# A twelve-sublayer decoder on one core: a written order of four engines for the fourth sublayer, loads by group in the first, and the channel attention's scores at the end of a drain step

## The chip, the cores and the metric

The kernel runs on one core of a Trainium2 chip. Five engines take part, each with an instruction queue of its own that it works through in order: TensorE (PE, with its weight loads shown as PEld), VectorE (DVE), ScalarE (ACT), GpSimd (POOL) and SyncE (SP), which here only issues DMA transfers. They wait for each other through semaphores. The metric is the device time of one execution in microseconds (us), the median of several runs. The profiler records one more execution; its span is the time from the first to the last instruction.

## The reference

A decoder of four layers with three sublayers each works on 64 sequences of 64 tokens with 256 features, 4096 tokens in all, next to a context of the same shape. Each sublayer is followed by a residual add and a layer norm. All is float32 unless said otherwise. Only these four sublayers matter here (`_softmax` and the casts left out):

```
x = _layernorm(x + L0_attn(x))        # 1: 16 query heads of 16, one key and value head, causal
    q = x @ q_w.T + q_b;  k = x @ k_w.T + k_b;  v = x @ v_w.T + v_b
    attn = softmax(where(causal, -inf, q k^T / 4));  out = (attn v) @ o_w.T + o_b
x = _layernorm(x + L0_xattn(x, ctx))  # 2: channel attention, no weights
    scaled = einsum('bsd,bse->bde', x, ctx) / 16
    attn = softmax(scaled, axis=1);  out = einsum('bde,bse->bsd', attn, ctx)
x = _layernorm(x + L0_ffn(x))         # 3: silu(x Wg) * (x Wu), then Wd; integer weights with scales
x = _layernorm(x + L1_attn(x))        # 4: attention over the 128 channels of one head
    k = x @ Wk + bk;  v = x @ Wv + bv                   # (64, 128) for each sequence
    scores = v k^T / 128;  attn = softmax(scores)       # per sequence, 64 x 64
    out = (attn v), repeated for 16 heads;  out = out @ Wo + bo
```

The sixteen heads of sublayer 4 are copies of one another, so the kernel adds the sixteen blocks of Wo once and multiplies by their sum (`wo`). Sublayers 5 to 12 are left as they are by the change.

## The kernel before

**Tiling.** Tokens are cut into 8 groups of 512 (NTOK), and each group into 4 tiles of 128 rows (TG), a tile being two sequences. X[g] holds a group's activations in SBUF during the whole program. CT[g] is the context transposed, `cns[g]` the context by rows. Weights and the context rows take slots of a ring of 8 buffers of 128 x 2048 numbers (`weight`, L323): a slot can be taken again when its last reader is done.

**Who sets the order.** A planner lays every engine's queue at compile time by its own estimate of costs. Inside `with self.tc.manual_schedule(engines=...)` the named engines keep the order of the program text. The first sublayer (`l0_attn`, L706) and the second and third, which run as one (`l0_both`, L839), name PE, ACT, DVE and POOL. The fourth (`l1_attn`, L980) names PE alone: ACT, DVE and POOL are laid by the planner there. SP is named nowhere. The next one, `l1_xattn`, names PE, ACT and DVE; everything from `l1_ffn` on names PE alone.

**Loads.** `run` (L351) issues all at the start in this order: x of group 0, the weights of the first sublayer, x of groups 1 to 7, ctxT of all groups. `l0_attn` then loads the row `l0_ob` and, through `context` (L742), the context rows of all groups. The transfers go through SP's queue. Each x, ctxT and ctx load of a group moves 512 KB.

**First sublayer.** Steps i = 0 to 37 work on 32 tiles, each tile in several stages: `scores` at step i, `probabilities` at i+1 (DVE sums, POOL multiplies at L649), `turned` at i+2 (PE transposes `pt`, ACT copies), `values` and `output` at i+3, `ended` at i+4. `prepare(g+1)` is spread over the four steps of group g in four parts; its `keys_values` sends v through a DMA to the other half of the partitions (`vs`, L600), and `queries` lets POOL add the bias row (`xb`, L605) and copy v and vs into `vbd` (L610). When the tiles are used up (i from 32) the steps of the drain already hold the channel attention of group 0: `next_scores`, `next_divided`, `next_values`, four tiles, a step each. `next_scores` writes the PSUM tile `s` of which there is one, DVE takes the maximum (L483), and ACT the exponentials (L489). It stands near the start of a step, ahead of `values`.

**Third sublayer.** `l0_both` goes through 48 units (8 groups of 6 slices of the hidden layer): `hidden(u)`, `down(u - 2)`, and between them the channel attention of the next group. At steps 36 and 39 DVE adds the blocks of Wo (`l1_output_weight`, L877).

**Fourth sublayer.** For each group: `rows_turned` (8 transposes into two banks, one copied by ACT, one by DVE; POOL adds the bias row to X as `xb`, L915), `keys_values` (kT and vT, L925, ACT adds the biases), `scores` (L936, a mask added by a bf16 matmul, DVE maximum, four ACT exponentials with row sums; `v` is vT turned), `turned` (pt, DVE copies), `values` (ot, ACT copies), `output` (o, L972, in two PSUM banks for four tiles; DVE makes z = o * sm + xb tile by tile, L974, then bn_stats, bn_aggr), and the norm: DVE L228, POOL's power -1/2 (L230), DVE nmr (L286), four ACT applies into X[g] (L288). PE's text order of a step is xt(i), pt(i-2), s(i-1), v(i-1), kv(i), ot(i-2), o(i-2): three groups are in flight. The banks: three shared by xt, pt, v and ot (`tr`), two `kv`, one `s`, two `acc`. Then `l1_xattn` begins with matmuls on rows that went through DRAM (L1046, L327), whose results DVE reduces (L1078).

Of the kernel before, what the change touches and what calls it, by code (L numbers as in the profile page):

```python
# [195 lines left out]
class Decoder:  # L196
# [154 lines left out]
    def run(self, layers):  # L351
        tc, nc, ctx = self.tc, self.nc, self.ctx
        self.const = self.pool(ctx, "const", 1)
        self.smallp = self.pool(ctx, "small", 4)
        self.xpool = self.pool(ctx, "xpool", 1)
        self.ring = self.pool(ctx, "ring", 8)

        self.X, self.CT, self.l3_rows = [], [], []
        for g in range(self.n_groups):
            xg = self.xpool.tile([P, TG, D], F32, tag=f"x{g}", name=f"x{g}")  # L360
            self.load(xg, self.ins["x"][g * NTOK : (g + 1) * NTOK, :].rearrange("(t p) d -> p t d", p=P))
            self.X.append(xg)
            if g == 0:
                self.l0_weights()
        self.constants()
        for g in range(self.n_groups):
            ct = self.xpool.tile([P, 2, NTOK], F32, tag=f"ct{g}", name=f"ct{g}")
            self.load(
                ct, self.ins["ctxT"][:, g * NTOK : (g + 1) * NTOK].rearrange("(c p) n -> p c n", p=P)
            )  # L370
            self.CT.append(ct)

        steps = [
            self.l0_attn, self.l0_both, self.l1_attn, self.l1_both,
            self.l2_l3, self.l3_xattn, self.l3_ffn,
        ]
        for n in layers:
            with ExitStack() as lctx:
                self.psum = self.pool(lctx, f"psum{n}", 2, space=PSUM, reuse_waits="tile")
                steps[n](lctx)  # L380
        for g in range(self.n_groups):
            for t in range(TG):
                at = g * NTOK + t * P
                nc.sync.dma_start(out=self.out[at : at + P, :], in_=self.X[g][:, t, :])

# [146 lines left out]
    def l0_attn(self, ctx):  # L532
# [161 lines left out]
        self.cns = [self.context(g) for g in range(self.n_groups)]  # L694
# [11 lines left out]
        with self.tc.manual_schedule(engines={E.PE, E.Activation, E.DVE, E.Pool}):  # L706
# [3 lines left out]
            for i in range(n + TG + 2):  # L710
# [3 lines left out]
                if i < n:  # L714
                    g, t = tiles[i]
                    if t == 0 and g + 1 < self.n_groups:
                        parts = prepare(g + 1)
                    state[i, "s"] = scores(g, t)
                elif i < n + TG:
                    next_scores(0, i - n)  # L720
                if 1 <= i <= n:
                    probabilities(state[i - 1, "s"])
                elif n < i <= n + TG:
                    next_divided(0, i - n - 1)
# [6 lines left out]
                if i < n:  # L731
                    exponentials(state[i, "s"])
                if behind:
                    behind()
                if 3 <= i <= n + 2:
                    state[i - 3, "ps"] = output(*tiles[i - 3], state.pop((i - 3, "o")))
                if i >= n + 2:
                    ends.extend(next_values(0, i - n - 2))
            for part in ends:
                part()  # L740

    def context(self, g):  # L742

        if g % 2 == 0:
            self.cn = self.weight("cn").rearrange("p (g t d) -> p g t d", g=2, t=TG)
        cn = self.cn[:, g % 2]
        self.load(cn, self.ins["ctx"][g * NTOK : (g + 1) * NTOK, :].rearrange("(t p) d -> p t d", p=P))
        return cn

    def l0_both(self, ctx):  # L750
# [88 lines left out]
        with self.tc.manual_schedule(engines={E.PE, E.Activation, E.DVE, E.Pool}):  # L839
            turn(0)  # L840
            for u in range(-1, len(units) + 2):
# [15 lines left out]
                if u in (HC * 6, HC * 6 + 3):  # L857
                    self.l1_output_weight(u == HC * 6)
            for part in ends:
                part()  # L860
# [15 lines left out]

    def l1_output_weight(self, first):  # L877
# [3 lines left out]
        if first:  # L881
            nc.vector.tensor_reduce(wo, raw[0], AX.X, ALU.add)
        else:
            nc.vector.tensor_reduce(half, raw[1], AX.X, ALU.add)
            nc.vector.tensor_tensor(wo, wo, half, ALU.add)

    def l1_attn(self, ctx):
# [3 lines left out]
        nc, ins = self.nc, self.ins  # L891
        DH = 128
        wk = self.pool(ctx, "l1a", 2)
# [3 lines left out]
        ident = wk.tile([P, P], BF16, tag="ident", name="ident", bufs=1)  # L897
        nc.vector.tensor_copy(ident, self.ident)
        mask = wk.tile([P, TG, P], BF16, tag="mask", name="mask", bufs=1)
        nc.vector.tensor_copy(mask, self.same.unsqueeze(1).broadcast_to([P, TG, P]))  # L900
        flat = lambda a: a.rearrange("p t n -> p (t n)")
        state = {}
# [4 lines left out]
        def rows_turned(g):  # L907
            xt = wk.tile([P, 2, NTOK], F32, tag="xt", name="xt")
            for c, copy in enumerate((nc.scalar.copy, nc.vector.tensor_copy)):
                ps = ring("xt")  # L910
                for t in range(TG):
                    nc.tensor.transpose(ps[:, t * P : (t + 1) * P], self.X[g][:, t, c * P : (c + 1) * P], self.ident)
                copy(xt[:, c, :], ps)
            xb = wk.tile([P, TG, D], F32, tag="xb", name="xb", bufs=3)
            nc.gpsimd.tensor_tensor(xb, self.X[g], bo.unsqueeze(1).broadcast_to([P, TG, D]), ALU.add)  # L915
            state[g] = xt, xb

        def keys_values(g):
            xt, xb = state[g]
            out = []  # L920
            for name, w_, b_ in (("kT", wkk, bk), ("vT", wvv, bv)):
# [5 lines left out]
                out.append(t_)  # L927
            state[g] = *out, xb

        def scores(g):  # L930

            kT, vT, xb = state[g]
# [6 lines left out]
            nc.tensor.matmul(ps, ident, flat(mask), start=False, stop=True, skip_group_check=True)  # L939
            s, sm = wk.tile([P, TG, P], F32, tag="s", name="s"), self.small(TG, "sm4")  # L940
            self.softmax_rows(s, ps.rearrange("p (t i) -> p t i", t=TG), TG, 1.0 / DH, sm)
            nc.vector.reciprocal(sm, sm)
# [5 lines left out]
            state[g] = s, sm, v, xb  # L948

        def turned(g):  # L950
            ps = ring("pt")
            for t in range(TG):
                nc.tensor.transpose(ps[:, t * P : (t + 1) * P], state[g][0][:, t, :], self.ident)
            pt = wk.tile([P, TG, P], F32, tag="pt", name="pt")
            nc.vector.tensor_copy(flat(pt), ps)
            return pt

        def values(g, pt):
            v, ps = state[g][2], ring("ot")
# [4 lines left out]
            return ot  # L964

        def output(g, ot):
            _, sm, _, xb = state.pop(g)
            z = wk.tile([P, TG, D], F32, tag="z", name="z")
            for t in range(TG):
                if t % 2 == 0:  # L970
                    ps = self.psum.tile([P, 2, D], F32, tag="acc", name="o", bufs=2)
                nc.tensor.matmul(ps[:, t % 2, :], ot[:, t * P : (t + 1) * P], wo, start=True, stop=True)  # L972

                nc.vector.scalar_tensor_tensor(  # L974
                    z[:, t, :], ps[:, t % 2, :], sm[:, t : t + 1], xb[:, t, :], ALU.mult, ALU.add
                )
            self.normalized(self.X[g], z)

        n = self.n_groups
        with self.tc.manual_schedule(engines={mybir.EngineType.PE}):  # L980
            for i in range(n + 2):
                if i < n:
                    rows_turned(i)
                if i >= 2:
                    pt = turned(i - 2)
                if 1 <= i <= n:
                    scores(i - 1)
                if i < n:
                    keys_values(i)
                if i >= 2:  # L990
                    output(i - 2, values(i - 2, pt))
# [1247 lines left out]
```

## Time and profile before

| what | us |
|---|---|
| median of 3 runs | 4510.14 |
| lowest and highest | 4506.65 and 4511.18 |
| the profiled execution's own time | 4513.13 |
| its span | 4511.4 |
| first sublayer, to the last step of its tiles (0 to 226.70) | 226.7 |
| its drain with the first channel attention (226.70 to 262.40) | 35.7 |
| second and third sublayer (262.40 to 605.80) | 343.4 |
| fourth sublayer, to its last apply (605.80 to 741.50) | 135.7 |
| PE busy in the whole span | 4118.9 (91%) |
| DVE, ACT, POOL busy | 3091.6, 2018.8, 1474.4 |

The profile has several views. The page gives busy times and groups of instructions. The timeline of an engine gives its instructions in order of time: start, duration, engine, line of the kernel (L...), operation, output<-input and shapes, and in brackets how long the engine had been idle before it and what released it. The windows view gives busy time of every engine in chosen stretches. PEclk is the share of PE's full clock that was granted. A float32 matmul shows as two instructions, so a group's four transposes of one kind can appear as x4 or x8.

### The profile page before, as it was taken

To read this page: it belongs to the slowest core of one execution; us is meant where nothing else is said; L and a number is where in the kernel's file an instruction comes from. 1 tells how busy PE (TensorE), PEld (TensorE's weight loads), DVE (VectorE), ACT (ScalarE), POOL (GpSimd) and SP (SyncE) were. 2 spreads that over 40 slices of the span, in tenths; PEclk is the share of its full clock that TensorE was granted. 3 is DMA by queue.
4 is the path that set the end of the run, shared out by engine and by line. 5 is a ranking of instruction groups with operands and counts; after the bars stand their busy time and mean duration, and the time that the engine had idled before them with its cause. 6 is when DMAs were issued, how large, how long until landed. Compare 5 with 4: busy or idle time off the path is not lost. (4 is left out here: it accounts for less than half of the span.)

```text
span 4511.4 us, 73874 instructions
## 1 busy us (share of the span) xinstructions
PE 4118.9 (91%) x28808; PEld 2662.9 (59%) x28808; DVE 3091.6 (69%) x6222; ACT 2018.8 (45%) x3662; POOL 1474.4 (33%) x1498
## 2 busy tenths in 40 slices
PE   7989988989988999839999999999979999999898
PEld 4645555666665555526666666666646666666566
DVE  5844536888665577767777777777757776777676
ACT  4655533767523566534444444444423322233444
POOL 3411111132431111015555555555523333333111
PEclk8989997999999999969999999999989999999999
DMA  4000011333200000011111111111210000000000
GB/s 142 3 20 10 5 48 33 69 82 69 65 1 21 1 1 1 10 47 29 27 27 29 27 27 29 24 29 29 65 56 10 10 10 10 10 11 12 7 16 17
DMA packets 99685, 128.26 MB, mean 28 GB/s; under 512 B 14916, under 2 KB 72452, under 8 KB 97928
## 3 DMA queue, kind: packets, MB, share of 16 engines
q1 hardware_dynamic: 99336, 123.53, 10.9%
q8 instruction: 228, 3.74, 0.3%
q14 instruction: 121, 0.99, 0.1%
HBM read 61.87 MB, written 19.42 MB: 18 GB/s over the span
## 5 line engine op out<-in xcount | busy, mean ns | idle before, releaser
L230 POOL TENSOR_TENSOR hrq<-hrq,neg_half 128x4 f32<-128x4 f32 x256 | 270.7, 1058 | 512.4 <-DVE hrq L228 512.3
L230 POOL TENSOR_TENSOR rstd<-rstd,neg_half 128x4 f32<-128x4 f32 (+1 forms) x168 | 148.2, 882 | 684.6 <-DVE rstd L228 599.3
L1078 DVE TENSOR_REDUCE mc<-sq 128x2 f32<-128x512 f32 x512 | 317.1, 682 | 64.2 <-PE sk L1076 63.6
L1084 ACT ACTIVATE e<-sk 128x512 f32<-128x512 f32 x512 | 265.2, 607 | 112.8 <-PE sk L1076 111.9
L230 POOL TENSOR_TENSOR hrk<-hrk,neg_half 128x4 f32<-128x4 f32 x160 | 187.8, 1174 | 291.0 <-DVE hrk L228 280.6
L1073 PE MATMUL sq<-l1x 32*128 32x256 f32 x2048 | 275.4, 406 | 1.6 <-DVE mc L1078 1.6
L1580 PE MATMUL p<-l3a_wq,xt 128*128 128x512 f32 x512 | 244.4, 601 | 9.9 <-DVE v L217 9.9
L1076 PE MATMUL sk<-l1x 32*128 32x256 f32 x2048 | 252.6, 393 | 0.5 <-DMA l1x<-l1x_m 0.5
L1580 PE MATMUL p<-l3x_wq,xt 128*128 128x512 f32 x512 | 238.2, 609 | 13.9 <-DVE k L1889 13.7
L1580 PE MATMUL p<-l3a_wk,xt 128*128 128x512 f32 x512 | 247.2, 606 | 0.0
L1073 PEld LDWEIGHTS sq<-l1x 32*128 32x128 f32 x2048 | 209.1, 194 | 55.4 <-issue 24.5
L1970 PE MATMUL acc<-l3x_wo,yt 128*128 128x256 f32 x1024 | 238.0, 386 | 0.7 <-ACT yt L215 0.7
L1580 PE MATMUL p<-l3a_wv,xt 128*128 128x512 f32 x512 | 234.5, 601 | 0.8 <-DVE k L217 0.4
L1787 PE MATMUL acc<-l3a_wproj,yt 128*128 128x256 f32 x1024 | 232.6, 381 | 0.0
L1787 PEld LDWEIGHTS acc<-l3a_wproj,yt 128*128 128x128 f32 x1024 | 195.1, 191 | 52.8 <-issue 29.1
L1970 PEld LDWEIGHTS acc<-l3x_wo,yt 128*128 128x128 f32 x1024 | 189.6, 190 | 28.0 <-ACT yt L215 0.9
L1076 PEld LDWEIGHTS sk<-l1x 32*128 32x128 f32 x2048 | 188.8, 187 | 7.2 <-issue 2.5
L1881 ACT ACTIVATE sq<-q 128x512 f32<-128x512 f32 x128 | 80.7, 630 | 207.3 <-DVE q L1889 154.4
L1580 PEld LDWEIGHTS p<-l3x_wq,xt 128*128 128x128 f32 x512 | 97.7, 196 | 126.6 <-issue 116.3
L1771 POOL TENSOR_TENSOR hry<-hry,neg_half 128x8 f32<-128x8 f32 x64 | 106.2, 1659 | 193.4 <-DVE hry L1767 193.4
L236 PEld LDWEIGHTS qT<-ident,q 128*128 128x128 f32 x1024 | 119.1, 141 | 77.3 <-issue 64.6
L1112 PE MATMUL ret<-e,vt 128*32 128x256 f32 x2048 | 140.5, 390 | 19.6 <-DVE mc L1078 18.6
(383 smaller groups left out, 10247.2 us busy)
## 6 DMA issues: line engine op xcount, KB each, us to landing
vs<-v SPq DMA_DIRECT2D x320, 128.0 KB
x<-in_x SPq DMA_DIRECT2D x8, 512.0 KB
ct<-in_ctxT SPq DMA_DIRECT2D x8, 512.0 KB
cn<-in_ctx SPq DMA_DIRECT2D x8, 512.0 KB
l1x<-in_ctx SPq DMA_DIRECT2D x128, 32.0 KB
l1x_x<-x SPq DMA_DIRECT2D x8, 512.0 KB
l1x<-l1x_x SPq DMA_DIRECT2D x128, 32.0 KB
l1x_r<-r SPq DMA_DIRECT2D x128, 32.0 KB
```

The costliest lines, as they stand in the source:

```text
L230: nc.gpsimd.tensor_tensor(out, out, self.neg_half[:, :n], ALU.pow)
L236: self.nc.tensor.transpose(ps[:, j * P : (j + 1) * P], blk, self.ident)
L1073: nc.tensor.matmul(ps[:, n, :], x_[rows, j, part], c_[rows, j, :], start=True, stop=True)
L1076: nc.tensor.matmul(ps[:, n, :], c_[rows, j, part], x_[rows, j, :], start=True, stop=True)
L1078: nc.vector.tensor_reduce(mc[new % 2][:, ra + k, 2 * j : 2 * j + 2], ps, AX.X, ALU.max, negate=True)
L1084: nc.scalar.activation(es[rb + k], ps, AF.Exp, scale=scale)
L1112: nc.tensor.matmul(ret[32 * r : 32 * r + 32, :], vt[i % 2][:, lc, 4 * r + j, :], es[r][:, lc, :], start=lc == 0, stop=lc == 1,)
L1580: self.nc.tensor.matmul(ps, lhs(c), w(c, cols), start=c == 0, stop=c == 1 and bias is None)
L1771: nc.gpsimd.tensor_tensor(r, r, self.neg_half[:, :8], ALU.pow)
L1787: nc.tensor.matmul(acc[:, :D], yts[h % 2][:, h // 2, :], wp[n // 8][:, (n % 8) * D : (n % 8 + 1) * D], start=n == 0, stop=n == 15,)
L1881: nc.scalar.activation(sq, x, AF.Square)
L1970: nc.tensor.matmul(acc[:, :D], yts[h % 2][:, h // 2, :], wo[n // 8][:, (n % 8) * D : (n % 8 + 1) * D], start=n == 0, stop=n == 15,)
```

## The change

**Fourth sublayer.** Its four engines (PE, ACT, DVE, POOL) now follow the text. A step i holds, in this order: the applies of an earlier group's norm (DVE nmr first, ACT after the turn), `l1_turn(i+1)` (the transposes of the next group), `turned(i-2)`, `scores(i-1)`, the second half of the sums of group i-4, `keys_values(i)`, `output(i-3)` with the first half of its sums, `values(i-2)`. So five groups are in flight instead of three, a group's output comes one step after its values, and its z, bn_stats and bn_aggr are split in two halves on two steps. xb is added on POOL in `turned`, the reciprocal is taken there too, and which engine copies which half of the transposed rows is swapped. The loop has n + 4 steps instead of n + 2. The turned rows live in a ring slot of their own (`l1_xt`, two groups), taken in `l1_weights`; group 0 is turned in step 48 of the third sublayer. The bf16 identity and mask move into the weight slot and are made in step 36 of the third sublayer.

**First sublayer, loads.** At the start only x of groups 0, 1 and 2 are loaded, around the weights. SP joins the engines of the written order, and at the third tile of group g it issues x of group g+3, ctxT of group g and the context rows of group g.

**First sublayer, drain.** `next_scores` goes from the start of a drain step to its end, behind `output` and `next_values`.

```diff
         self.X, self.CT, self.cns, self.l3_rows = [], [], [], []
...
+        self.load_rows(0)
+        self.l0_weights()
+        for g in (1, 2):
+            self.load_rows(g)
         self.constants()
-        for g in range(self.n_groups):
-            ct = self.xpool.tile([P, 2, NTOK], F32, tag=f"ct{g}", name=f"ct{g}")
-            self.load(
-                ct, self.ins["ctxT"][:, g * NTOK : (g + 1) * NTOK].rearrange("(c p) n -> p c n", p=P)
-            )
...
+    def load_rows(self, g):
+        if g < self.n_groups:
+            self.load(self.X[g], self.ins["x"][g * NTOK : (g + 1) * NTOK, :].rearrange("(t p) d -> p t d", p=P))
+
+    def load_context(self, g):
+        rows = slice(g * NTOK, (g + 1) * NTOK)
+        self.load(self.CT[g], self.ins["ctxT"][:, rows].rearrange("(c p) n -> p c n", p=P))
+        if g % 2 == 0:
+            self.cn = self.weight("cn").rearrange("p (g t d) -> p g t d", g=2, t=TG)
+        self.cns.append(self.cn[:, g % 2])
+        self.load(self.cns[g], self.ins["ctx"][rows, :].rearrange("(t p) d -> p t d", p=P))
...
-        self.cns = [self.context(g) for g in range(self.n_groups)]
...
-        with self.tc.manual_schedule(engines={E.PE, E.Activation, E.DVE, E.Pool}):
+        with self.tc.manual_schedule(engines={E.PE, E.Activation, E.DVE, E.Pool, E.SP}):
...
                     state[i, "s"] = scores(g, t)
-                elif i < n + TG:
-                    next_scores(0, i - n)
...
                     exponentials(state[i, "s"])
+                    if t == 2:
+                        self.load_rows(g + 3)
+                        self.load_context(g)
...
                 if i >= n + 2:
                     ends.extend(next_values(0, i - n - 2))
+                if n <= i < n + TG:
+                    next_scores(0, i - n)
...
+                if u == len(units):
+                    self.l1_turn(0, lambda: self.bank("xt", tag="gu", bufs=3))
...
+        self.l1_ident, self.l1_mask = w[:, 1024:1088].bitcast(BF16), w[:, 1088:1344].bitcast(BF16)
+        self.l1_xt = self.weight("l1_xt").rearrange("p (i c n) -> p i c n", i=2, c=2)
...
+    def l1_turn(self, g, bank):
+        nc, xt = self.nc, self.l1_xt[:, g % 2]
+        for c, copy in enumerate((nc.vector.tensor_copy, nc.scalar.copy)):
+            ps = bank()
+            for t in range(TG):
+                nc.tensor.transpose(ps[:, t * P : (t + 1) * P], self.X[g][:, t, c * P : (c + 1) * P], self.ident)
+            copy(xt[:, c, :], ps)
...
+        def sums(g, half):
+            z, pss, sm, xb = state[g, "z"]
+            if half == 0:
+                state[g, "mv"] = self.smallp.tile([P, TG, 2], F32, tag="bnmv", name="bnmv", bufs=4)
+            for i in range(2):
+                t = 2 * half + i
+                st = self.smallp.tile([P, 6], F32, tag="bnst1", name="bnst1", bufs=4)
                 nc.vector.scalar_tensor_tensor(
+                    z[:, t, :], pss[half][:, i, :], sm[:, t : t + 1], xb[:, t, :], ALU.mult, ALU.add
                 )
+                nc.vector.bn_stats(st, z[:, t, :])
+                nc.vector.bn_aggr(state[g, "mv"][:, t, :], st)
+            if half == 1:
+                del state[g, "z"]
+                ends.extend(self.group_end(state, g, self.X[g], z))
...
-        with self.tc.manual_schedule(engines={mybir.EngineType.PE}):
-            for i in range(n + 2):
-                if i < n:
-                    rows_turned(i)
-                if i >= 2:
-                    pt = turned(i - 2)
-                if 1 <= i <= n:
-                    scores(i - 1)
-                if i < n:
-                    keys_values(i)
-                if i >= 2:
-                    output(i - 2, values(i - 2, pt))
+        with self.tc.manual_schedule(engines={E.PE, E.Activation, E.DVE, E.Pool}):
+            for i in range(n + 4):
+                behind = ends.pop(0) if ends else None
+                if i + 1 < n:
+                    self.l1_turn(i + 1, lambda: ring("xt"))
+                if behind:
+                    behind()
+                if 2 <= i <= n + 1:
+                    turned(i - 2)
+                if 1 <= i <= n:
+                    scores(i - 1)
+                if i >= 4:
+                    sums(i - 4, 1)
+                if i < n:
+                    keys_values(i)
+                if 3 <= i <= n + 2:
+                    output(i - 3)
+                    sums(i - 3, 0)
+                if 2 <= i <= n + 1:
+                    values(i - 2)
+            for part in ends:
+                part()
```

## The prediction

> **What bounds the kernel now.** The chain that ended last was read first; its pieces all lie beyond 4,200 us, so it says nothing of the places that the change touches. I therefore cut the span into stretches at the instructions that open each sublayer and asked for the busy time of each engine in them (columns: length, then busy time and count for PE, PEld, DVE, ACT, POOL; then PE's granted clock, DMA share, GB/s):
>
> ```profile
> 0.00:46.40 46.40, 19.55 (x173) 12.53 (x173) 11.53 (x16) 9.80 (x13) 10.32 (x40) 0.81 1.01 331
> 46.40:226.70 180.30, 164.55 (x2552) 116.09 (x2553) 140.90 (x218) 107.24 (x181) 85.16 (x78) 0.98 0.03 6
> 226.70:262.40 35.70, 22.47 (x188) 13.56 (x188) 16.82 (x45) 15.53 (x49) 8.83 (x12) 0.81 0.12 33
> 262.40:605.80 343.40, 333.22 (x1281) 178.83 (x1282) 156.17 (x363) 184.08 (x387) 38.94 (x74) 0.99 0.04 14
> 605.80:741.50 135.70, 101.09 (x424) 67.42 (x424) 58.30 (x168) 53.55 (x141) 28.05 (x17) 0.79 0.13 40
> ```
>
> Rows two and four run close to PE's limit (91% and 97%). The other three do not: row one is the load of the inputs (the DMA engines are full), row three the drain of the first sublayer, row five the fourth sublayer, where no engine is full and PE's clock is 0.79. Those three are what the change edits. For row one, the timelines of SP, POOL and PE:
>
> ```profile
> 22.71 13.03 SPq L327 DMA_DIRECT2D cn<-in_ctx  x8
> 31.33 2.34 POOL L605 TENSOR_TENSOR xb<-x,l_ob 128x1024 f32<-128x1024 f32 x1 [24.56 <-DMA cn<-in_ctx]
> 43.64 0.52 POOL L610 COPY vbd<-vs 64x64 f32<-64x64 f32 x2 [9.81 <-DMA vs<-v]
> 44.42 1.90 POOL L649 TENSOR_TENSOR s<-s,sm 128x1024 f32<-128x1024 f32 x1
> 46.38 1.97 PE L236 MATMUL pt<-ident,s 128*128 128x128 f32 x8 [19.83 <-POOL s L649]
> ```
>
> POOL's queue stands at xb and at the vbd copies, because the row of l0_ob lies behind 8 MB of x and ctxT in the DMA queue and the half swap vs behind another 4 MB of ctx; PE then idles 19.83 us for POOL. For row five, the same windows by group, then PE's timeline of the fast kind:
>
> ```profile
> 662.90:676.10 13.20, 9.71 (x50) 6.57 (x50) 6.71 (x19) 6.25 (x17) 3.39 (x2) 1.00 0.12 41
> 676.10:691.10 15.00, 12.46 (x50) 8.69 (x50) 6.33 (x19) 6.15 (x17) 3.37 (x2) 0.77 0.10 36
> ```
>
> ```profile
> 666.38 1.04 PE L912 MATMUL xt<-ident,x 128*128 128x128 f32 x8
> 667.25 0.60 PE L953 MATMUL pt<-ident,s 128*128 128x128 f32 x4
> 667.69 1.06 PE L936 MATMUL s<-kT,vT 128*128 128x128 f32 x8
> 668.58 0.38 PE L939 MATMUL s<-mask,ident 128*128 128x512 bf16 x1
> 668.80 0.60 PE L945 MATMUL v<-ident,vT 128*128 128x128 f32 x4
> 669.23 3.60 PE L925 MATMUL kv<-xt,l1a 128*128 128x512 f32 x8
> 672.67 1.05 PE L961 MATMUL ot<-pt,v 128*128 128x128 f32 x8
> 676.06 0.70 PE L972 MATMUL o<-l1a,ot 128*128 128x256 f32 x2 [2.34 <-ACT ot L963]
> 677.34 2.08 PE L972 MATMUL o<-l1a,ot 128*128 128x256 f32 x4 [0.58 <-DVE z L974]
> ```
>
> PE, whose order is written, stands in each group at o: ACT has put the applies, exponentials, kT and vT ahead of the copy ot; then o waits twice for DVE's z to free its bank.
>
> **The fourth sublayer, step by step.** PE's work for one group, from start to start in these rows: xt 0.87, pt 0.44, s 0.89, mask 0.22, v 0.43, kv 3.44, ot 0.86, and o four times 0.43 = 1.71; together 8.9 us against 13.2 to 15.3. In the new order each of these has its input from an earlier step: o(i-3) uses the ot copied a step before, its two banks are freed by the sums of the two halves, v(i-1) needs only vT. I walked the four queues through one step with the durations of the rows: ACT 6.7 us (xt 0.58, applies 2.07, exponentials 1.4, v 0.58, kT and vT 1.38, ot 0.58), DVE 7.1 (xt 0.69, pt 0.66, the maximum 0.69, four times z, bn_stats, bn_aggr at 1.05, small ones 0.7), POOL 3.4 (xb 2.36, pow 1.01). All are under 8.9 and the tightest hand-over, ot's copy at the end of ACT's step before the next pt in the same ring, has about 0.1 us. So PE sets the step; with the 97% that row four reaches in a written order, 9.15.
>
> Begin and end in that walk. PE is free at 605.8 as before. ACT's first work stands behind the third sublayer's last applies (610.6 to 612.7, unchanged), so kT(0) is made near 613.3, s(0) starts at 614.9 instead of 621.1, and the dense steps begin at 627.7. Steps 3 to 7 at 8.9 (the last without xt) end at 671.2. Then kv and xt are gone and DVE sets the pace: 6.2, 5.4 and 4.6 us for steps 8 to 10, and the last half sum, pow and applies end at 694.3. Before, the last applies (739.35, 2.08) ended at 741.4, and DVE's first l1x reduction stood behind them (741.92). This gate stays. Stretch: 88.5 us, plus 5 x 0.25 for the 97%, plus the clock.
>
> The clock: the rows above drop to 0.77 after single waits of 2.3 us, and the old drain (718.90 to 730.90), after one of 3.74, has 0.50. [...] by the rows its twelve o products (0.43 each) run at half speed on the path of three groups: +1.3 us. I take the row. 88.5 + 1.2 + 1.3 = 91.0 against 135.6: -44.6.
>
> [...] rstd (L228) took 0.87 us beside xb, 0.17 without. [...] by the row 0.7 x 8 = 5.6. In the walk xb follows pow directly and runs while DVE waits for o, and DVE has 1.7 us to spare in a step, so I charge nothing and keep 5.6 as the bad end.
>
> The third sublayer now also turns group 0 (8 transposes, 0.87 on a PE that is 97% full), and DVE gets the two casts in step 36 (0.23, and about 0.5 for the mask, by the 0.29 us of the half as wide L548; its 2.58 before was beside xb): +0.9 and +0.5. The copies of the turn hide behind the last down products. The fourth ring slot held through the sublayer (l1_xt) makes one later weight, l1_wd, wait for a slot until about 672 to 687; it is used past unit 48 of the next sublayer, far later. If SP kept it ahead of the stores of X, the first l1x rows would land near 694, which is just the gate: 0, at worst 5 us.
>
> **The loads.** Ahead of l0_ob there are now x0, the weights (0.66 MB), x1 and x2: 2.3 MB with itself, at the 355 GB/s of the full rows some 7 us, so l0_ob is there near 9.5 and xb ends near 12. v is ready at 13.0, vs lands some 2 to 3 us later; if SP still puts the 2.1 MB of the next sublayer's weights in front, 6 more: 22. Both are before DVE's reciprocal of the first tile (25.63 to 25.88), which then sets POOL's product (1.90) and pt at 27.9: 18.5 us earlier. PE then waits 1.4 instead of 19.83 us and stays warm: the next projection takes 1.98 instead of 3.78, and DVE's reduction of tile 3 comes at 32.6 instead of 53.35, 20.7 earlier. I take -20; ends -14 and -21. The moved loads (8 ctxT, 8 ctx, 5 x, 0.5 MB each) go out three per group, 1.5 MB or 4.3 us of DMA in a group of 25 us, after the same group's vs in SP's order; the next vs is due two steps later and x(g+3) six steps later, so nobody waits. Without that slack it would be those 4.3 us per group.
>
> **The drain of the first sublayer.** Before, the channel attention's scores for tile 0 start at 226.72, then 234.15, 242.05, 251.61, and the last value product at 258.27. The loop is scores 2.08, DVE 1.40, ACT 1.80, ot copy 0.38, o 2.08: the ot copy stands behind ACT's exponentials. At the end of the step the first scores must wait for pt of tile 30 (POOL's product, 230.15), 1.1, and o, 1.5: 232.8 instead of 226.7. The loop is the same ring entered elsewhere: 240.9, 250.9 (the first value product now lies in it), 256.4, and the last value product at 263.0. That is a loss of 4.7; the first sublayer's own outputs come 1.3 earlier and nobody waits for them. Ends: -1 to +6. The turn of the third sublayer waits for it, so I charge +4.7.
>
> **Sum.** -20 + 4.7 + 1.4 - 44.6 = -58.5 us. On the profiled span of 4511.4 that gives 4453; the run was 4513.1 with 1.7 around the span, and the median is 4510.1: **4452**.
>
> **Rivals.** (B) The four queues lock into each other and a step takes 11 us, half-way to 13.2: 7 steps x 2.1 = +15, 4467; at 13.2 it is +30, 4482. For it: 0.1 us at the ring of three banks; against: the third sublayer's 97%. (C) Planned loads keep l0_ob or vs late: up to +20, 4472. (D) On the other side: only PE's order is written from the fifth sublayer's ffn on (1230 to 4511, 3281 us); ACT, DVE and POOL there are laid by the planner, whose plan starts from other slots and times. If those stages stretch by 3%, +98: 4550; it decides from 58.5/3281 = 1.8%. Against it: their program is untouched and they are mostly PE-full. (E) The order does nothing and the period stays: only -15 remains, 4495.
>
> **Numbers.** The likeliest case has 0.72 (own range 4438 to 4466), B 0.12, C 0.08, D 0.05, E 0.03. 4436 to 4482 leaves out D, E and thin edges. A change of 0.2% (9 us) is what can be told from none. Faster: all of A to C and most of E, 0.94; the same 0.02; slower 0.04.
>
> **What would show it.** Right: pt of the first tile near 28; l1 steps of about 9 us with the clock at 1.00 and o with waits under 0.3; the last applies some 45 us nearer to the third sublayer's end; the last value product of the first drain some 42 us after the scores of tile 31 (37 before). Wrong: xb or vbd still waiting for a DMA; DVE or ACT busy over 85% in the dense steps; l1x's first reduction held by its rows instead of the applies; or stages past 1230 of other lengths.

## The result and the profile after

The changed kernel takes 4455.4 us (median of 4 runs, 4446.41 to 4460.64) against 4508.4 us of the kernel before (4 runs, 4506.49 to 4511.18): a ratio of 0.988 with a 95% interval of 0.9862 to 0.9898. The forecast was 4452 us. The profiled execution took 4457.41 us with a span of 4455.7, which is 55.7 us less than the span before.

The same view as before the change, busy time by stretch, cut at the same events (columns: length; busy time and count of PE, PEld, DVE, ACT, POOL; granted clock; DMA share; GB/s):

```profile
0.00:28.00 28.00, 20.43 (x173) 12.81 (x173) 8.40 (x13) 9.80 (x13) 10.28 (x40) 0.94 0.36 92
28.00:205.80 177.80, 161.79 (x2556) 114.58 (x2556) 143.59 (x221) 107.12 (x180) 85.19 (x78) 1.00 0.23 77
205.80:246.70 40.90, 24.25 (x189) 14.34 (x188) 17.73 (x46) 15.70 (x49) 8.84 (x12) 0.73 0.11 29
246.70:590.10 343.40, 334.04 (x1288) 179.62 (x1288) 154.75 (x363) 184.86 (x388) 38.89 (x74) 0.98 0.02 7
590.10:686.60 96.50, 80.56 (x417) 59.01 (x416) 60.78 (x168) 53.67 (x140) 27.71 (x17) 0.93 0.26 83
```

The loads and the dense part of the first sublayer lost 20.9 us (226.7 to 205.8), its drain gained 5.2, the second and third sublayer stayed at 343.4, the fourth lost 39.2. That is 54.9 of the 55.7; the rest, 0.8, lies in the 3,769 us behind.

The start, in the timelines of SP, POOL and PE of the kernel after. xb still waits for a transfer, but only until 12.53 instead of 31.33; the swap vs goes out at 12.94, and POOL's product now waits for DVE's sums. PE waits 0.62 us for it instead of 19.83:

```profile
12.94 1.16 SPq L609 DMA_DIRECT2D vs<-v  x2
12.53 2.34 POOL L614 TENSOR_TENSOR xb<-x,l_ob 128x1024 f32<-128x1024 f32 x1 [5.77 <-DMA l_u<-in_l_u]
15.47 0.23 POOL L619 COPY vbd<-vs 64x64 f32<-64x64 f32 x1 [0.25 <-DMA vs<-v]
26.01 1.90 POOL L658 TENSOR_TENSOR s<-s,sm 128x1024 f32<-128x1024 f32 x1 [10.13 <-DVE sm L657]
27.97 1.09 PE L236 MATMUL pt<-ident,s 128*128 128x128 f32 x8 [0.62 <-POOL s L658]
```

A step of the fourth sublayer, PE's timeline of the kernel after, from one turn of the rows to the next (the rows of pt, s, mask and v are left out): 8.99 us (8.92 to 8.99 in all dense steps), at a granted clock of 1.00, with no wait in brackets anywhere. The waits of each group before (one for ACT's copy, two for z) are gone:

```profile
635.54 1.04 PE L905 MATMUL xt<-ident,x 128*128 128x128 f32 x8
638.48 3.60 PE L932 MATMUL kv<-l_xt,l1a 128*128 128x512 f32 x8
641.91 1.89 PE L983 MATMUL o<-l1a,ot 128*128 128x256 f32 x8
643.64 1.05 PE L972 MATMUL ot<-pt,v 128*128 128x128 f32 x8
644.53 1.04 PE L905 MATMUL xt<-ident,x 128*128 128x128 f32 x8
```

What the forecast did not have is at the two ends of that sublayer. At its begin, the timelines of DVE, POOL and PE:

```profile
588.71 0.91 DVE L1062 MEMSET l1x<- 128x1024 f32 x1 [0.16 <-issue]
596.26 0.17 DVE L228 TENSOR_SCALAR rstd<-bnmv 128x4 f32<-128x4 f32 x1
597.49 2.34 POOL L964 TENSOR_TENSOR xb<-x,l_bo 128x1024 f32<-128x1024 f32 x1
597.55 2.29 DVE L464 SCALAR_TENSOR_TENSOR nmr<-bnmv,rstd 128x4 f32<-128x4 f32 x1 [1.12 <-POOL rstd L230]
600.50 1.11 PE L905 MATMUL xt<-ident,x 128*128 128x128 f32 x4 [5.43 <-DVE l_xt L906]
603.70 2.07 PE L942 MATMUL s<-kT,vT 128*128 128x128 f32 x8 [2.08 <-ACT vT L933]
```

Four memsets of the next stage's rows (the first is shown) stand between the last sums of the third sublayer and delay rstd (596.26, 8.07 us after the start of the last down product; 5.73 with the memsets on POOL, below). In the kernel before they ran in the middle of that sublayer, at 459.14, 542.91, 545.72 and 564.99; DVE's timeline of the last:

```profile
564.99 0.91 DVE L1027 MEMSET l1x<- 128x1024 f32 x1 [0.16 <-issue]
```

Then nmr, 4 numbers for each partition and 0.16 us before the change, starts and ends with POOL's xb beside it. The first scores come 15.5 us after the start of the last down product (588.19), 13.5 after its end, where the forecast had 9.1.

Three stretches are used below. *Drain*: from PE's score products of tile 31 in the first sublayer to the third sublayer's first turn (before 41.3 us, after 45.9; the table's rows are cut elsewhere, hence 5.2 there and 4.6 here). *Turn*: from the start of the last down product to the first scores of the fourth sublayer (after 15.5). *Fourth*: from the same start to the first reduction of the stage behind (before 138.1, after 98.8).

### The profile page after: what moved, and what is told of

It is laid out like the page before. It is cut to its first block, busy times and chain, and to the rows that moved or that the text cites. A ratio compares the mean times of both kernels' runs of the same rounds, so it can differ in the third digit from the quotient of the medians.

```text
span 4455.7 us, 73891 instructions
## 1 busy us (share of the span) xinstructions
PE 4100.9 (92%) x28808; PEld 2654.3 (60%) x28808; DVE 3094.2 (69%) x6222; ACT 2020.9 (45%) x3662; POOL 1473.9 (33%) x1498
## 5 line engine op out<-in xcount | busy, mean ns | idle before, releaser
L1615 PE MATMUL p<-l3x_wq,xt 128*128 128x512 f32 x512 | 238.9, 610 | 13.2 <-DVE k L1924 13.0
```

The lines of the kernel that those rows point to most:

```text
L1615: self.nc.tensor.matmul(ps, lhs(c), w(c, cols), start=c == 0, stop=c == 1 and bias is None)
```

## The experiments

All were timed beside the kernel before, which took 4509 to 4510 us in these comparisons. Differences of a few us are judged by the stretches of the traces, since runs of one program scatter by up to 14 us. The stages behind the fourth sublayer, which no edit touches, took 3761.3 to 3771.5 us in the traces, so that much of this scatter is theirs.

### Loads alone

The kernel before, with the load hunks of the change and SP in the written order, nothing else:

```diff
+        for g in (1, 2):
+            self.load_rows(g)
...
+                    if t == 2:
+                        self.load_rows(g + 3)
+                        self.load_context(g)
```

> The kernel before with the loads of the first sublayer alone by group (SP's queue written too); channel scores, third and fourth sublayer as before. My theory: the first product of the probabilities comes at 27.9 us instead of 46.4 and everything behind it 20 to 21 us earlier, with nothing given back: 4508 - 20 = 4488 us. The last value product of the channel attention's tile 0 follows the scores of tile 31 by 37 us, as before. Rival 1: the shift is not carried through, because the stages behind are laid out by the planner and stretch: 4500 us or more. Rival 2: the loads cost the dense part of the sublayer its slack (1.5 MB in each group of 25 us), 1 us a group: 4496 us.

4489.83 us (4486.66 to 4491.92), ratio 0.9956 (0.9939 to 0.9972): 19.3 us. In its trace, PE:

```profile
27.53 1.97 PE L236 MATMUL pt<-ident,s 128*128 128x128 f32 x8 [1.46 <-POOL s L658]
236.48 1.44 PE L522 MATMUL o<-s,pt 128*64 128x256 f32 x8 [0.75 <-POOL pt L512]
```

The first pt is at 27.5, and the last value product of the drain comes at 236.48, 21.8 us earlier than before. It follows the scores of tile 31 by 34.6 us (counted from their mask product), less than the 37 of the kernel before. A part of the 21.8 is thus the clock of this one drain (0.89 granted instead of 0.83; the channel scores of the four tiles took 1.13, 1.13, 1.13 and 2.08 us instead of 1.14, 2.08, 1.81 and 2.08). The span is 24.9 us shorter than that of the kernel before, of which 3.4 lie in the far later stages (3766.1 instead of 3769.5), as much as equal programs differ there. The gain is carried through, so rival 1 falls, and the dense part costs nothing, so rival 2 falls.

### Does SP's written order matter?

The changed kernel with SP left to the planner:

```diff
-        with self.tc.manual_schedule(engines={E.PE, E.Activation, E.DVE, E.Pool, E.SP}):
+        with self.tc.manual_schedule(engines={E.PE, E.Activation, E.DVE, E.Pool}):
```

> The changed kernel without SP's queue in the written order of the first sublayer: the program still names the loads by group, but the planner places them, 1.5 MB ahead of the first half swap vs, another 6 MB ahead of the second. Theory (swaps have slack of two steps in group 0 and six behind): POOL's product still waits for DVE and the first pt comes near 28 us; 0 in all, 4455 us. Rival (the written queue is what keeps vs early): the second or third swap is late, POOL's vbd copies stand again, and 5 to 20 us are lost in the first 100 us: 4460 to 4475 us.

4455.98 us (4451.9 to 4463.31), ratio 0.9881 (0.9866 to 0.9896). SP's and PE's timelines:

```profile
12.83 1.16 SPq L609 DMA_DIRECT2D vs<-v  x2
25.80 1.49 SPq L609 DMA_DIRECT2D vs<-v  x2
27.82 1.76 PE L236 MATMUL pt<-ident,s 128*128 128x128 f32 x8 [1.46 <-POOL s L658]
```

The planner issues all the moved loads by 37 us, and still the swaps go out at 12.83 and 25.80, no later than in the changed kernel (12.94 and 26.57). So the 20 us come from what stands ahead of l_ob and of the first swap, not from spreading the rest over the sublayer.

### The place of the channel scores

The changed kernel with next_scores at the begin of the step again:

```diff
                     state[i, "s"] = scores(g, t)
+                elif n <= i < n + TG:
+                    next_scores(0, i - n)
...
-                if n <= i < n + TG:
-                    next_scores(0, i - n)
```

> The changed kernel with one thing undone: the channel attention's scores stand at the begin of a drain step again. My theory: the drain is 4.6 us shorter (the last value product follows the scores of tile 31 by 37 us instead of 41.6), all else as in the changed kernel: 4455.4 - 4.6 = 4451 us. Rival 1: the place of the scores costs nothing, because the sublayer's own outputs then end 1.3 us later and the next sublayer's turn waits for them: 4455 us. Rival 2: with the new loads the late place is the better one: 4458 us.

4448.38 us (4447.93 to 4450.04), ratio 0.9864 (0.9849 to 0.9879), 7.0 us under the changed kernel. PE's timeline of the changed kernel first, then of this one:

```profile
212.18 2.08 PE L488 MATMUL s<-x,cn 64*128 64x256 f32 x8
241.68 2.32 PE L522 MATMUL o<-s,pt 128*64 128x256 f32 x8 [2.72 <-POOL pt L512]
247.32 2.80 PE L801 MATMUL xt<-ident,x 128*128 128x128 f32 x8 [3.31 <-ACT x L466]
```

```profile
207.54 1.13 PE L488 MATMUL s<-x,cn 64*128 64x256 f32 x8 [0.61 <-DVE s L647]
236.62 1.43 PE L522 MATMUL o<-s,pt 128*64 128x256 f32 x8 [0.75 <-POOL pt L512]
241.37 2.80 PE L801 MATMUL xt<-ident,x 128*128 128x128 f32 x8 [3.32 <-ACT x L466]
```

The drain takes 38.9 us instead of 45.9. With all the traces of this study the size is better seen: the five with the old place have 41.3 (before), 38.8, 38.9, 39.3 and 39.3, mean 39.5; the eight with the new place 45.9, 45.9, 44.4, 43.5, 43.4, 42.8, 42.7 and 42.7, mean 43.9. The place costs 4.4 us on average. The scatter inside each set, some 3 us, goes with PE's clock: over the eight, the granted clock of the stretch is 0.75 and 0.76 in the two of 45.9 us, 0.80 in the one of 44.4, 0.82 in the two near 43.5 and 0.85 in the three near 42.7; the channel scores of the four tiles took 8.0 us together in the first two, 6.5 in the next one, 5.4 in the two near 43.5 and 4.9 to 5.0 in the last three. One reason for the cost can be read from the rows: at the old place the scores fill a wait. Before the pt of tile 31 PE stands 1.67 us for POOL in this kernel (at 210.93) and 3.42 in the changed one (at 209.85). Both rivals fall: the next turn does follow the last value product.

### Written order or depth?

First, the changed kernel with TensorE alone written in the fourth sublayer:

```diff
-        with self.tc.manual_schedule(engines={E.PE, E.Activation, E.DVE, E.Pool}):
+        with self.tc.manual_schedule(engines={E.PE}):
             for i in range(n + 4):
```

> The changed kernel, but in the fourth sublayer only TensorE's order is written; ACT, DVE and POOL are laid by the planner again, with the same five groups in flight. Theory (depth does it: o takes a copy made a step before): steps of 8.9 to 9.5 us, 4455 to 4460 us. Rival (the written order of ACT and DVE does it: the planner puts applies and exponentials ahead of the copies again): steps of 11 to 13 us, 4470 to 4485 us.

4448.72 us (4445.8 to 4452.68), ratio 0.9865 (0.985 to 0.988): better than both theories said. The dense steps are 8.93 to 8.99 us, the turn 15.5, both as in the changed kernel; but the fourth stretch is 94.0 us instead of 98.8, and all of these 4.8 us lie behind the last turn of rows (which stands 40.8 us after the first scores in both). So the planner's orders serve the deep pipeline just as well and empty it faster.

Second, written orders with one group less in flight:

```diff
-            for i in range(n + 4):
+            for i in range(n + 3):
...
-                if i >= 4:
-                    sums(i - 4, 1)
+                if i >= 3:
+                    sums(i - 3, 1)
...
-                if 3 <= i <= n + 2:
-                    output(i - 3)
-                    sums(i - 3, 0)
                 if 2 <= i <= n + 1:
                     values(i - 2)
+                    output(i - 2)
+                    sums(i - 2, 0)
```

> The changed kernel, but with one group less in flight in the fourth sublayer: the output products stand in the same step as the value products they take, and the orders of all four engines stay written. Theory (depth does it): o waits about 0.9 us in each step for the copy ot, which stands behind kT and vT on ACT; steps of 9.8 instead of 8.95 us, 7 us in all, of which one drain step of about 5 us comes back: 4457 us. Rival 1 (a written order alone is enough): steps of 8.95 us and one drain step less: 4450 us. Rival 2 (without the depth the queues lock as before): steps of 11 to 13 us, 4470 us or more.

4461.07 us (4457.95 to 4462.73), ratio 0.9891 (0.9876 to 0.9906). PE's timeline:

```profile
624.52 1.05 PE L972 MATMUL ot<-pt,v 128*128 128x128 f32 x8
626.25 1.99 PE L983 MATMUL o<-l1a,ot 128*128 128x256 f32 x8 [0.68 <-ACT ot L974]
628.08 1.04 PE L905 MATMUL xt<-ident,x 128*128 128x128 f32 x8
```

o waits 0.68 to 0.73 us for the copy ot in each step, and a step takes 9.85 to 9.90 us, as the first theory had it (9.8). The fourth stretch is 104.1 us, 5.2 more than with the depth of the change: at the last turn of rows this kernel is 5.5 us behind, and the way from there is only 0.3 shorter, not 5. Rivals 1 and 2 fall.

The last group of depth is thus worth 0.9 to 1.0 us of a step. It is not the whole gain. The fast step before (13.2 us) stood 2.5 us between ot and o, for the copy, and its o products took 3.5 us (662.86 to 666.38) instead of 1.7 because of the two stops for z (0.58 us idle ahead of each of the last two rows of o); together that is the 4.3 us above 8.9. The stops for z do not come back here: the four o run as one x8 row. In the text before, each z stood right behind its product, and the rows of the kernel before run x2, stop, x4, stop, x2 (a product is two instructions): the second product into each PSUM bank waited for the z of the first. The new text issues all four products and then the sums. This reading of the text fits both traces, but the z moved alone was not tried. Nor were the other differences between this kernel and the one before: the turn of the rows a step ahead, the sums in two halves, and the written orders at this depth.

### Which queue of the written order costs the drain 4.8 us?

DVE, or POOL, taken out of the written order alone:

```diff
-        with self.tc.manual_schedule(engines={E.PE, E.Activation, E.DVE, E.Pool}):
+        with self.tc.manual_schedule(engines={E.PE, E.Activation, E.Pool}):    # first kernel
+        with self.tc.manual_schedule(engines={E.PE, E.Activation, E.DVE}):     # second kernel
```

> The changed kernel with DVE taken out of the written order of the fourth sublayer alone (TensorE, ACT and POOL stay written). With TensorE's order alone the stretch from the start of the last down product to the first reduction of the next stage was 94.0 us instead of 98.8, all of it in the drain. Theory (DVE's written order puts a whole half of one group's sums ahead of the next's and so holds the o banks): 3.4 of the 4.8 us come back, 95.4 us. Rival (POOL's order does it: xb behind pow blocks nmr for 1.46 us and o waits 2.60 us in consequence): 98.8 us, nothing.

> The changed kernel with POOL taken out of the written order of the fourth sublayer alone; the planner then lays each xb ahead of the pow of two groups before. Theory (DVE's order has most of the loss): only the 1.46 us come back in which nmr stood behind xb in the drain, 97.4 us from the last down product's start to the next stage's first reduction. Rival (POOL's order does it all): 94.0 us, with nmr at 0.15 us and no o of the drain waiting over 1.2 us.

Without DVE 4448.85 us (4445.73 to 4448.87), ratio 0.9859 (0.9844 to 0.9874), the fourth stretch 96.0 us; without POOL 4456.56 us (4451.57 to 4460.74), ratio 0.9878 (0.9862 to 0.9895), 99.6 us. POOL's and DVE's timelines of the second, where xb stands ahead of pow:

```profile
661.08 2.36 POOL L964 TENSOR_TENSOR xb<-x,l_bo 128x1024 f32<-128x1024 f32 x1 [4.57 <-DVE z L994]
661.65 1.82 DVE L228 TENSOR_SCALAR rstd<-bnmv 128x4 f32<-128x4 f32 x1
665.49 0.13 DVE L464 SCALAR_TENSOR_TENSOR nmr<-bnmv,rstd 128x4 f32<-128x4 f32 x1
```

nmr is short again, but the hold has only moved to rstd (1.82 us instead of 0.17), so nothing came back (the stretch is 0.8 longer): the theory's 1.46 us were wrong here. Without DVE's written order 2.8 of the 4.8 us came back (3.4 expected), although nmr was then held for the whole of POOL's xb (POOL's and DVE's timelines):

```profile
662.07 2.35 POOL L964 TENSOR_TENSOR xb<-x,l_bo 128x1024 f32<-128x1024 f32 x1
662.13 2.31 DVE L464 SCALAR_TENSOR_TENSOR nmr<-bnmv,rstd 128x4 f32<-128x4 f32 x1
```

In both kernels the same hold (rstd 1.81 us, nmr 2.31) also stands in the dense steps, and these still take 8.93 to 8.99 us: there it costs nothing.

With both free (and ACT too), xb again runs ahead of pow, but DVE has the copy of pt, statistics and the next maximum to do beside it, which last as long as elsewhere (0.68, 0.42 and 0.69 us), and nmr is short; only the scaling of the maximum is held, for 0.67 us; the timelines of POOL, DVE and PE with TensorE's order alone:

```profile
660.75 2.37 POOL L964 TENSOR_TENSOR xb<-x,l_bo 128x1024 f32<-128x1024 f32 x1 [4.27 <-DVE z L994]
664.86 0.16 DVE L464 SCALAR_TENSOR_TENSOR nmr<-bnmv,rstd 128x4 f32<-128x4 f32 x1
666.92 1.13 PE L983 MATMUL o<-l1a,ot 128*128 128x256 f32 x4 [0.51 <-DVE z L994]
```

In the changed kernel the same place reads, for DVE and PE:

```profile
668.55 1.46 DVE L464 SCALAR_TENSOR_TENSOR nmr<-bnmv,rstd 128x4 f32<-128x4 f32 x1
672.17 2.08 PE L983 MATMUL o<-l1a,ot 128*128 128x256 f32 x4 [2.60 <-DVE z L994]
```

o waits 2.60 us for a bank that DVE's sums free, behind a held nmr, and then takes 2.08 us, where the same x4 row took 1.13 at 668.44. DVE's order is the larger part. The other 2.0 us belong to POOL's order, to ACT's, or to both: POOL's alone gave nothing back, and ACT's was not tried.

### The memsets and the held nmr at the begin

The memsets of the l1x rows on POOL:

```diff
         for t in xr:
-            nc.vector.memset(t, 0.0)
+            nc.gpsimd.memset(t, 0.0)
```

> The changed kernel with the four memsets of the l1x rows on POOL instead of DVE. Theory: they stand on DVE between the last bn_stats of the third sublayer and hold its rstd for 2.9 us (four of 0.91, less what DVE waits there anyhow); on POOL they run before its pow. The first scores of the fourth sublayer come 12.6 us after the start of the last down product instead of 15.5, and the whole is 2.9 us shorter: 4452 us, or by the profile's stretches -2.9 +/- 0.5. Rival: the gap at the turn is set by ACT's applies and the turn of the second half, so the memsets only fill a wait: 0.

4454.66 us (4453.35 to 4456.91), ratio 0.9878 (0.9861 to 0.9894). Medians can't tell this from the changed kernel; the trace can. The turn is 12.66 us (600.80 - 588.14) instead of 15.51, the 2.9 expected; the fourth stretch is 96.5, 2.3 less. POOL and PE:

```profile
582.93 3.63 POOL L1062 MEMSET l1x<- 128x1024 f32 x4
600.80 2.08 PE L942 MATMUL s<-kT,vT 128*128 128x128 f32 x8 [5.33 <-ACT vT L933]
```

xb of group 0 on DVE:

```diff
-            nc.gpsimd.tensor_tensor(xb, self.X[g], bo.unsqueeze(1).broadcast_to([P, TG, D]), ALU.add)
+            on = nc.vector if g == 0 else nc.gpsimd
+            on.tensor_tensor(xb, self.X[g], bo.unsqueeze(1).broadcast_to([P, TG, D]), ALU.add)
```

> The changed kernel with the bias sum xb of group 0 on DVE instead of POOL. Theory (DVE's small nmr is held off for as long as POOL's 128x1024 sum runs, 2.29 us instead of 0.16): nmr takes under 0.3 us, the first scores of the fourth sublayer come 13.4 us after the start of the last down product instead of 15.5: -2.1 us, of which DVE's own xb (about 1.1 us, in a gap) gives nothing back: 4453 us. Rival: nmr is long for another reason (its input from POOL's pow lands late) and stays long: 0.

4450.31 us (4448.7 to 4454.05), ratio 0.9868 (0.9853 to 0.9883). DVE and PE:

```profile
598.38 0.16 DVE L464 SCALAR_TENSOR_TENSOR nmr<-bnmv,rstd 128x4 f32<-128x4 f32 x1 [1.12 <-POOL rstd L230]
602.39 2.08 PE L942 MATMUL s<-kT,vT 128*128 128x128 f32 x8 [2.54 <-ACT vT L933]
```

nmr takes 0.16 us with the same input at the same distance behind pow, and the turn is 13.38 us, the 13.4 expected. The rival is out: it was POOL's instruction that held it. The fourth stretch is 97.2 us, 1.6 less.

### Together

The old place of the scores, TensorE's order alone in the fourth sublayer, the memsets on POOL, xb of group 0 on DVE:

> Four edits to the changed kernel together: the channel scores back at the begin of the drain step, only TensorE's order written in the fourth sublayer, the l1x memsets on POOL, xb of group 0 on DVE. Theory: they lie at different places and add up, 7 (or 4.6, the place where the clock decides) + 4.8 + 2.9 + 2.1: 4455 - 16 = 4439 us, ends 4436 and 4443. Rival: the planner, which lays ACT, DVE and POOL again, gives a part back at the turn: 4447 us, no better than one of them alone.

4438.26 us (4431.01 to 4445.18), ratio 0.984 (0.9825 to 0.9854): 17.1 us under the changed kernel, 16 expected. The turn is 10.5 us and the fourth stretch 89.0, 9.8 less than in the changed kernel: 2.9 + 2.1 + 4.8 = 9.8. The drain is 39.3. The rival, a planner that gives a part back at the turn, falls. In the traces these two stretches are 16.4 us shorter than in the changed kernel; another 7.4 us of this execution lie in the stages behind, whose program is the same, and are chance. The result beats both kernels.

Its trace showed two more stops on the way to the first probabilities, and both were taken away:

```diff
-            on = nc.vector if g == 0 else nc.gpsimd
+            on = nc.vector if g < 2 else nc.gpsimd
...
+            if g == 0:
+                nc.scalar.activation(self.small(1, "early", bufs=1), t_[:, :1], AF.Exp)
```

> The four edits of the best kernel so far (4438 us), with two more at the begin of the fourth sublayer: a small exponential right behind vT of group 0, so that ACT loads its table while it waits (1.28 us between the first maximum and the first exponential), and xb of group 1 on DVE too (POOL's xb ran while DVE scaled the first maximum: 1.42 us instead of 0.17). Theory: both lie one behind the other on the path from the first scores to the first probabilities: -1.3 - 1.2 = -2.5 us, 4435.7 us; the first pt 5.5 us after the first scores' start instead of 8.2. Rival (TensorE has other work there and the dense steps begin no earlier): 4438 us.

4437.01 us (4436.81 to 4440.75), ratio 0.9837 (0.9822 to 0.9851). First a line of DVE in the four-edit kernel, then ACT, DVE and PE with the two more:

```profile
595.30 1.42 DVE L300 TENSOR_SCALAR nb<-nb 128x4 f32<-128x4 f32 x1
```

```profile
593.43 1.28 ACT L936 ACT_TABLE_LOAD   x1
595.30 0.17 DVE L300 TENSOR_SCALAR nb<-nb 128x4 f32<-128x4 f32 x1
595.18 4.74 PE L932 MATMUL kv<-l_xt,l1a 128*128 128x512 f32 x8
599.76 1.04 PE L905 MATMUL xt<-ident,x 128*128 128x128 f32 x8
```

Both stops are gone, and the fourth stretch is 89.0 us as before, to the hundredth. PE has the projection kv of group 1 and the next turn in its order ahead of pt, until 600.6. In the four-edit kernel the exponentials ended at 598.74 and pt began at 600.81: the probabilities were not late there either. The first pt comes 7.65 us after the first scores in both (5.5 expected). The rival had it: a wait cleared behind an engine that has other work first is worth nothing.

## Why the prediction was right, and where it was wrong

The time fell 3.4 us above the forecast, inside its range, and by the mechanism named in the main. Some of the nearness is luck: a miss of 5.4 us in the fourth sublayer was in part covered by 1.4 us charged for nothing in the third and 0.9 more from the loads. By its steps:

- **Loads, -20.** Right: 20.9 in the stretches, 19.3 alone. pt at 27.97 against 27.9, and the projection behind it took 1.98 us instead of 3.78. One sign of being wrong did appear, xb waiting for a transfer, until 12.5 where the forecast had 9.5; POOL's product stood behind DVE's sums until 26.0, so it cost nothing. Rival C (planned loads late) didn't come up, and the run with a planned SP shows that it needn't have been SP's order that prevents it.
- **Drain, +4.7.** Right in sign and mean (4.4 over all traces), 4.6 in this trace. Of these, 3.7 lie ahead of the last value product; the rest is behind it, and that product took 2.32 us instead of 1.44. The change would have been better without this part.
- **Third sublayer, +1.4.** Measured 0: 343.4 us both times. The turn of group 0 and the two casts fit into what was idle.
- **Fourth sublayer, -44.6.** Measured -39.2: this is the term that was mis-sized. The step was right (8.92 to 8.99 against 8.9; 9.15 with the 97%). In a step of 8.99 us DVE and ACT were busy 6.5 and 6.4 us and POOL 3.4, where the walk had 7.1, 6.7 and 3.4; the walk's own items add to 6.9 and 6.6. The step's reason, an input from an earlier step for every product, holds for the copy ot: with less depth a wait of 0.68 to 0.73 us for it comes back in every step. That it is the split of the sums that frees the banks of o was not tried apart; it is not the depth, since with less of it they were no hindrance either. The walk's start, 9.1 us from the last down to the first scores, was 4.4 short: 2.9 for the four memsets, which the sum did not have at all, and 2.1 for nmr. With both taken away the first scores come 8.5 us after the last down's end, so the rest of the walk held. The way from there to the last apply was 82.8 us against 79.4 + 1.2 + 1.3 = 81.9. The ring slot that l1_xt keeps was weighed for one weight load only; that the planner's memsets of other slots of the same ring move into the gap was not thought of. That the slot is what moves them was only argued; it was not tried apart. The place of the scores, the written orders of ACT, DVE and POOL, and SP's are not the cause, since the turn is 15.5 us in the runs without them too.
- **DVE's hold beside xb at nothing.** Wrong choice. The walk argued that xb runs while DVE waits for o, and in the dense steps it does: nmr takes 0.15 us there. At the begin (2.29) and in the drain (1.46) it does not. The two exceed nmr's usual 0.15 by 3.5 us, between the 0 taken and the 5.6 kept as the bad end. Of these the 2.1 at the begin were on the path, as the run with xb of group 0 on DVE shows; a hold in each dense step would have cost nothing, as the two runs above show.
- **The clock in the drain, +1.3.** Right to charge it: the o at 672.17 took 2.08 us for half a group, 1.13 at 668.44, after a wait of 2.60 us, and the ot behind it took 1.72 instead of 1.05, about 1.6 us in that place (the granted clock from 671 to 676 was 0.66).
- **l1_wd, 0.** Right: the stage behind was released by the last applies, not by its rows.
- **Rivals B, D and E.** No step of 11 us; the stages behind took 3768.7 us against 3769.5.

The written order of ACT, DVE and POOL, which the forecast took as part of the gain, brought no gain that the planner doesn't match: TensorE's order with the same depth is 4.8 us better in its trace.

## What to carry to other kernels

The last group of depth took what was left of the copy's wait (0.68 to 0.73 us a step) off PE's path, and with this depth the written queues of the other engines were not needed: write the order of the engine that sets the pace, and give each of its products an input from a step before. Look at what stands between two products into one PSUM bank; a reader put there in the text seems to have stopped the second here (0.58 us idle, twice in a group; not tried apart). Look for what the change pushes into the gaps between two stages, since here four memsets (2.9 us) and a 4-wide instruction beside a 2.3 us one (2.1 us) were on the path there, while in the dense part the same hold cost nothing (steps of 8.93 to 8.99 us with rstd at 1.81 or nmr at 2.31). Before a wait is cleared, read what the pacing engine does at that time.

## What the runs showed of the hardware

**A small DVE instruction can last as long as POOL's large one.** Beside POOL's xb of 2.34 to 2.36 us, nmr took 2.29, rstd 1.82 and the scaling of the maximum 1.42 us, against 0.13 to 0.17 alone; each started 0.06 to 0.9 us after xb and ended within 0.03 us of its end. With group 0's xb off POOL, nmr took 0.16 us at the same distance behind pow. Not every DVE instruction was held: in the changed kernel z took 0.48 us at 643.05 with xb running from 642.52 to 644.88, and 0.48 at 639.05 without it. Moving POOL's instruction in its queue only changed the victim: without POOL's written order nmr took 0.13 us and rstd 1.82. Why some are held and others not was not shown.

**The same program has PE at full or at half speed at the same place.** Two programs that do not differ before the fourth sublayer, PE in the first drain, the changed kernel and then the one with less depth:

```profile
214.96 1.09 PE L236 MATMUL pt<-ident,s 128*128 128x128 f32 x8
218.08 2.08 PE L688 MATMUL o<-l0a,ot 128*128 128x256 f32 x4 [2.03 <-ACT ot L682]
```

```profile
216.56 1.09 PE L236 MATMUL pt<-ident,s 128*128 128x128 f32 x8
219.87 1.13 PE L688 MATMUL o<-l0a,ot 128*128 128x256 f32 x4 [2.21 <-ACT ot L682]
```

In both the pt ahead of the wait is at full speed (1.09 us; in the kernel before, at 46.38 behind a wait of 19.83, it takes 1.97). After the wait of 2.03 us the product takes 2.08 us, after the one of 2.21 us 1.13. So the length of the wait alone did not decide here. The eight drains with the new place of the scores, equal programs up to there, took from 42.7 to 45.9 us. What decides it was not shown.
